# A gated feed-forward and convolution kernel: LoRA products ahead of block 0's transposes, shared statistics, P1 in halves, and other places for the sums

## Chip, cores and metric

The kernel runs on one core of a Trainium2 chip. The metric is the device time of one execution in microseconds (us), the median of several runs. The engines are named as the profile names them: PE is TensorE (PEld its weight loads), DVE VectorE, ACT ScalarE, POOL GpSimd, SP SyncE, whose queue here only issues transfers.

## What is computed

x is 2 x 1024 rows of 512 float32 numbers. Shortened from the reference:

```python
def lora_linear(x, w, a, b):                       # rank 16, SCALING = 2
    return x @ w.T + (x @ a.T) @ b.T * SCALING

xn = layernorm(x)                                  # over the last axis, 512
s = convolve(xn, K) + D * xn                       # K: 512 taps, from 64 complex states
h1, h3 = lora_linear(xn, w1, A1, B1), lora_linear(xn, w3, A3, B3)   # 512 -> 1376
g = silu(h1) * h3
f = lora_linear(g, w2, A2, B2)                     # 1376 -> 512
out = x + s * silu(f)
```

Everything is float32. A product of a 128x128 block by 512 columns is two matmul instructions on PE.

## The kernel before

**Tiles.** The 2048 tokens are four blocks of 512 (TB), each of four tiles of 128. Two blocks form a superblock. The hidden size 1376 is five pairs of chunks (2 x 128, NPAIR) and a last chunk of 96 rows. LoRA is merged into the weights: small products of the rank-16 factors (lora_product, L362) go to a PSUM bank, and merge (L373) adds them to the weight tile on DVE. The factors lie in two halves of the hidden axis, split at 768 (LSPLIT).

**Fast matrix products.** The first layer is done with seven products in place of eight (a Strassen-Winograd form), over two levels for the pairs. A Chain (L719) is seven products P1 to P7 over sums of weights and sums of tokens; the order of the steps is that of the list PLACES (L41): P1, P6, P2, P7, P5, P3, P4. x, w and y are PSUM banks (two of each): P1 starts x, ACT copies x to w, P2 adds to w; P6 and P5 add to x, and ACT takes snapshots (21 and 22) of it; P7 starts y; total(22) adds y to snapshot 22 on DVE; P3 adds to x, P4 to y, and total(21) adds y to snapshot 21. So P4 may not start before total(22) has read y, and y comes free after total(21). Each pair has seven chains (pair_chains, L809; orders, L969), and the last chunk has one for each superblock (last_chain, L793). What a chain delivers is added to other chains' results (plus, L822: DVE for the h1 part, POOL for the h3 part); a Gate (L768) applies silu on ACT and multiplies on POOL, and store_g writes g to DRAM.

**Sums.** Token sums are made on DVE: outer_token_sum (L301, four for each superblock) and inner_token_sum (L317, four names, each for the raw part, raw=True, 1536 elements, and for the sums, 2048 elements). Weight sums: outer_weight_sums (L400) and inner_weight_sum (L409), on DVE; last_sums on POOL.

**Order of the work.** All of the first layer is laid out by hand on a time axis. at(place, what) puts a step into a heap, and after(delay, what) puts one behind the present place; the loop at L1179 takes the steps out in order of place and issues their instructions. One place is about one product of PE. Each engine works its instructions in that order and waits for what an instruction needs. add_chain (L897) puts the seven steps of chain n at 7n + place. SOON (L42) is PLACES with P4 at 11 and not at 13. SP's transfers are issued in the order in which the program has them, at most eight under way at a time.

**The beginning** (L909 to L956 and the first places). SP loads block 0's tiles, block 1, the last chunk's weights, pair 0, blocks 2 and 3, pair 1. ACT's queue issues four LoRA transfers of half 1, loads its function table (warm, L916), then issues those of half 0. PE multiplies the identity by itself (keep_warm, 24 products whose result nobody reads), makes the last chunk's LoRA products, more keep_warm, and transposes block 0 by two tiles. DVE makes the statistics of block 0 (norm_stats, L228), the inverse root (newton_rsqrt, L45: 10 steps, with norm_root's own two 12), then block 1's statistics. normalize (L272) works on ACT (tiles 0 and 2) and POOL (1 and 3). Then come P1 and P2 of the last chain, pair 0's LoRA products between them, block 1's transposes, and the first pair chain. Block 2's statistics are made on DVE at places -6 to -3.6, block 3's on ACT (act_sums, act_squares) with POOL.

**Second layer.** Eight units (unit, L1239) of two token tiles each read g back (load_g, L1078) and multiply with w2 in the same seven-product form; the first two run in turns (run, L1324). Their first product adds chunks of g in order; the last chunks land last. The convolution is multiplied in from unit 4 on.

## Time and profile before

| | us |
|---|---|
| median of three runs | 466.6 (466.06 to 467.17) |
| the profiled execution's own time | 465.92 |
| its span in the trace | 464.1 |
| PE busy | 451.9 |
| DVE busy | 290.3 |
| POOL busy | 194.4 |
| ACT busy | 136.3 |
| first matmul of a chain starts at | 14.26 |
| first matmul of the second layer starts at | 288.52 |

The granted clock of PE is 1.00 in the profile. Durations and places in time come from the one profiled execution, from the start of its span. In a row of the timeline the first number is the start, the second the length of the merged row, then engine, line, operation, what is written and read, and the shape; a bracket gives the engine's idle time before it and what released it. In a row of waits: who waited for whom, us in total, times, the longest. A row of windows has the stretch, its length, then busy time and count for PE, PEld, DVE, ACT and POOL, the granted clock, DMA share and GB/s. A line number can be that of a helper: L709 is every product of a chain.

### The profile page before, as it was taken

What the parts mean: (1) busy time and instruction counts of PE and PEld (TensorE: products, weight loads), DVE (VectorE), ACT (ScalarE), POOL (GpSimd) and SP (SyncE); (2) the same over time, 40 slices, a digit from 0 to 9 for tenths busy, and PEclk for the clock granted to TensorE, in tenths of its full rate; (3) what the DMA queues carried; (4) which work ended last, traced back from release to release, by engine and by line L of the source; (5) the groups of instructions that cost most, each with busy time, mean ns of one, the idle gap of its engine ahead of it and who ended that gap; (6) DMA issues with size and microseconds to landing.
All of it is one profiled execution on the core that took longest, in us unless ns stands there. A gap on an engine that the chain in (4) does not pass through costs nothing.

```text
span 464.1 us, 5003 instructions
## 1 busy us (share of the span) xinstructions
PE 451.9 (97%) x1682; PEld 274.9 (59%) x1682; DVE 290.3 (63%) x494; ACT 136.3 (29%) x281; POOL 194.4 (42%) x156
## 2 busy tenths in 40 slices
PE   8999898989999999999999999999999999999996
PEld 8635333334433443344333344888889898999895
DVE  5898979664776477547745586959786123442222
ACT  2675242433234334432442133111111101111110
POOL 2324262497559555945693359500000112222221
PEclk9999999999999999999999999999999999999999
DMA  8910312015102410241036229296901842422211
GB/s 249 359 43 18 130 57 84 0 54 174 46 23 69 137 45 23 69 151 44 23 98 220 80 83 269 91 333 214 347 1 47 287 139 91 137 90 92 80 57 45
DMA packets 35049, 53.36 MB, mean 115 GB/s; under 512 B 4528, under 2 KB 21168, under 8 KB 34896
## 3 DMA queue, kind: packets, MB, share of 16 engines
q1 hardware_dynamic: 34768, 52.74, 34.6%
q10 hardware_dynamic: 256, 0.31, 0.2%
q8 instruction: 13, 0.21, 0.2%
q14 instruction: 12, 0.10, 0.1%
HBM read 33.64 MB, written 19.40 MB: 114 GB/s over the span
## 4 chain that ended last, share of the span: by engine, by line
PE 83%; DVE 8%; DMA 3%; ACT 2%; POOL 2%; issue 1%; SPq 0%; POOLq 0%
PE x L709 39%; PE y L709 21%; PE w L709 11%; PE aux L881 6%; PE aux L364 2%; PE aux L489 2%; DMA room<-g_dram 2%; DVE s L419 1%; DMA s<-in_x_dram 1%; DVE xt L310 1%; DVE s L733 1%; DVE w L407 1%; DVE t_in L326 1%; POOL s L790 1%; PE w L881 1%
## 5 line engine op out<-in xcount | busy, mean ns | idle before, releaser
L1236 POOL TENSOR_TENSOR o<-o,xin 128x512 f32<-128x512 f32 (+1 forms) x17 | 22.5, 1324 | 140.1 <-DVE o L1235 140.1
L790 POOL TENSOR_TENSOR s<-c,s 128x512 f32<-128x512 f32 (+1 forms) x44 | 59.6, 1356 | 23.2 <-ACT c L782 20.7
L729 ACT COPY s<-x 128x512 f32<-128x512 f32 (+1 forms) x54 | 31.6, 586 | 95.4 <-PE x L709 95.2
L709 PE MATMUL x<-t_in,s 128*128 128x512 f32 (+1 forms) x148 | 56.5, 504 | 0.0
L733 DVE TENSOR_TENSOR s<-s,y 128x512 f32<-128x512 f32 (+1 forms) x54 | 36.5, 681 | 24.1 <-PE y L709 14.4
L823 POOL TENSOR_TENSOR ua_three<-ua_three,s 128x512 f32<-128x512 f32 x20 | 29.8, 1489 | 34.9 <-DVE s L733 34.9
L709 PEld LDWEIGHTS x<-t_in,s 128*128 128x128 f32 x148 | 26.4, 189 | 21.8 <-issue 13.8
L823 POOL TENSOR_TENSOR s<-ua_three,s 128x512 f32<-128x512 f32 x18 | 29.8, 1653 | 21.5 <-DVE s L733 21.5
L709 PE MATMUL y<-t_in,s 128*128 128x256 f32 (+1 forms) x108 | 36.2, 461 | 1.4 <-DVE s L733 1.4
L1257 ACT COPY z<-x 128x256 f32<-128x256 f32 x24 | 8.9, 373 | 83.5 <-PE x L709 83.5
L782 ACT ACTIVATE c<-c 128x512 f32<-128x512 f32 x40 | 25.1, 632 | 12.7 <-DVE c L823 12.7
L709 PEld LDWEIGHTS y<-t_in,s 128*128 128x128 f32 x108 | 20.0, 190 | 13.4 <-issue 8.5
L823 POOL TENSOR_TENSOR s<-u_three,s 128x512 f32<-128x512 f32 x20 | 26.6, 1332 | 0.8
L747 ACT COPY w<-x 128x512 f32<-128x512 f32 (+1 forms) x37 | 21.5, 581 | 8.5 <-PE x L709 8.5
L881 PE MATMUL aux<-conv,xr 128*128 128x128 f32 (+1 forms) x128 | 23.2, 314 | 0.0
L709 PE MATMUL x<-xt,w 128*128 128x512 f32 x40 | 21.0, 607 | 0.7 <-ACT w L747 0.7
L709 PE MATMUL x<-t_in,w 128*128 128x512 f32 x40 | 21.3, 613 | 0.4 <-ACT w L747 0.4
L823 POOL TENSOR_TENSOR u_three<-ua_three,u_three 128x512 f32<-128x512 f32 x10 | 13.3, 1326 | 19.8 <-DVE u_three L733 17.9
L709 PE MATMUL x<-xr,w 128*128 128x512 f32 x40 | 20.8, 615 | 0.6 <-ACT ua_three L729 0.5
L1234 DVE TENSOR_TENSOR aux<-aux,m 128x256 f32<-128x256 f32 x16 | 6.9, 431 | 23.1 <-PE aux L881 23.1
L709 PE MATMUL x<-xr,s 128*128 128x512 f32 x40 | 20.6, 614 | 0.7 <-ACT s L729 0.7
L709 PE MATMUL y<-xt,w 128*128 128x512 f32 x40 | 19.9, 595 | 1.4 <-DVE s L733 1.4
(271 smaller groups left out, 871.5 us busy)
## 6 DMA issues: line engine op xcount, KB each, us to landing
g_dram<-s SPq DMA_DIRECT2D x40, 256.0 KB, 2.1
g<-g_dram SPq DMA_DIRECT2D x10, 512.0 KB, 5.7
xin<-in_x_dram SPq DMA_DIRECT2D x16, 256.0 KB, 2.7
out_dram<-o SPq DMA_DIRECT2D x14, 256.0 KB, 2.0
t_in<-g_dram SPq DMA_DIRECT2D x6, 512.0 KB, 4.2
w<-in_w1T_dram SPq DMA_DIRECT2D x10, 256.0 KB, 3.6
w<-in_w3T_dram SPq DMA_DIRECT2D x10, 256.0 KB, 4.4
s<-in_x_dram SPq DMA_DIRECT2D x8, 256.0 KB, 4.2
```

The source lines that it names most:

```text
L364: nc.tensor.matmul(ps, lhsT=d[:, dc * P : (dc + 1) * P], rhs=h, start=start, stop=True, skip_group_check=True,)
L489: nc.tensor.matmul(ps, lhsT=h, rhs=d, start=True, stop=True)
L709: nc.tensor.matmul(ps, lhsT=lhsT, rhs=rhs, start=first and i == 0, stop=i == len(pairs) - 1, skip_group_check=True,)
L729: nc.scalar.copy(t, self.x)
L733: nc.vector.tensor_tensor(t, t, self.y, add)
L747: nc.scalar.copy(self.w, self.x)
L782: nc.scalar.activation(c, c if src is None else src, AF.Silu)
L790: nc.gpsimd.tensor_tensor(g, act, g, mult)
L823: (nc.vector if o < 20 else nc.gpsimd).tensor_tensor(to, a, b, add)
L881: nc.tensor.matmul(to, lhsT=x_, rhs=by, start=start, stop=True, skip_group_check=True)
L1236: (nc.vector if last else nc.gpsimd).tensor_tensor(o, o, self.xin[h][:, cols], add)
L1257: nc.scalar.copy(t, xb)
```

## The change

- The LoRA factors of half 1 are issued on ACT after the table load, those of half 0 on SP after all other loads. The pairs of the hidden axis are worked in a rotated order (PAIR_AT), and the first two then lie in half 1; w2 is loaded in three pieces in that order (CHUNK_AT).
- keep_warm: 12 products in place of 24 ahead of the LoRA products, 4 later in place of 11. The first LoRA group of pair 0 comes ahead of block 0's transposes, into banks x and w, and its second group between P1 and P2 of the last chain.
- Block 0's tile 1 gets its statistics on ACT and POOL (act_tile); DVE does the others. The inverse root has 8 steps in place of 10. Tile 0 is normalized on DVE.
- The first last chain's P1 is made in two halves of 256 tokens. Token sums of superblocks are made in two halves.
- Block 2's statistics go from places -6 to -3.6 to -1.4 to 1.1; two of block 3's squares to 1.7 and 1.8. P2 of the first pair chain goes from -1.8 to -6.
- In pair 0 the chains 2 to 5 use PLACES in place of SOON. Token sums 1 and 4 of superblock 1, the inner token sums, pair 1's outer weight sums and all inner weight sums 2 and 4 go to later places.
- The gate of the one chain that is held back (early3) and the h3 sum into it go from POOL to DVE.
- At the end of the first layer the P4 of one chain goes from place 13 to 13.5; the first two units of the second layer leave the last chunk of their first product to a second step (wait).

The diff, cut to its core:

```diff
+PAIR_AT = [2 * P * ((c + 3) % NPAIR) for c in range(NPAIR)]
+CHUNK_AT = [PAIR_AT[fc // 2] + fc % 2 * P for fc in range(LAST)] + [LAST * P]
...
-def newton_rsqrt(nc, pool, v, shape):
+def rsqrt(nc, pool, v, shape):
...
-        y.bitcast(I32), v.bitcast(I32), -0.5, float(0x5F3759DF), ALU.mult, ALU.add
+        y.bitcast(I32), v.bitcast(I32), -0.5, float(0x5F1FFFF9), ALU.mult, ALU.add
     )
-    for _ in range(3):
-        nc.vector.tensor_tensor(t, y, y, ALU.mult)
-        nc.vector.scalar_tensor_tensor(t, t, -0.5, v, ALU.mult, ALU.mult)
-        nc.vector.scalar_tensor_tensor(y, t, 1.5, y, ALU.add, ALU.mult)
+    nc.vector.tensor_tensor(t, y, y, ALU.mult)
+    nc.vector.scalar_tensor_tensor(t, t, -c2, v, ALU.mult, ALU.mult)
+    nc.vector.scalar_tensor_tensor(y, t, c2 * 2.38924456, y, ALU.add, ALU.mult)
+    nc.vector.tensor_tensor(t, y, y, ALU.mult)
+    nc.vector.scalar_tensor_tensor(t, t, 1.0 / part**2, v, ALU.mult, ALU.mult)
+    nc.vector.scalar_tensor_tensor(t, t, -10.0 / 3.0, t, ALU.add, ALU.mult)
+    nc.vector.scalar_tensor_tensor(y, t, 5.0, y, ALU.add, ALU.mult)
...
+    def act_tile(b, tt):
+        one = slice(tt, tt + 1)
+        act_sums(b, tt)
+        act_means(b, one)
+        act_squares(b, tt)
+        act_variances(b, one)
...
-                nc.gpsimd.tensor_scalar(t, t, rstd[:, one], shift[:, one], mult, add)
+                engine = nc.vector if tt in on_vector else nc.gpsimd
+                engine.tensor_scalar(t, t, rstd[:, one], shift[:, one], mult, add)
...
-        nc.vector.tensor_tensor(t[name - 1], one, other, add if name == 2 else sub)
+        for k in range(2):
+            to, a, b = (v[:, k] for v in (t[name - 1], one, other))
+            nc.vector.tensor_tensor(to, a, b, add if name == 2 else sub)
...
+            engine = nc.vector if early3 else nc.gpsimd
...
-                        plus(o, held[o], held[o], ua)
+                        nc.vector.tensor_tensor(held[o], held[o], ua, add)
...
-            return Chain(pairs, P, keep, got)
+            return Chain(pairs, P, keep, got, 0.7 if (c, j) == (NPAIR - 1, order[5]) else 0)
...
+    nc.scalar.activation(warm, warm, AF.Silu)
     load_lora(factors, nc.scalar, (1,))
-    nc.scalar.activation(warm, warm, AF.Silu)
-    load_lora(factors, nc.scalar, (0,))
...
     w_pair[1] = load_pair(1)
+    load_lora(factors, nc.sync, (0,))
...
-        keep_warm(ps, 12, True)
+        keep_warm(ps, 6, True)
     ps_last = lora_last()
+    merge_pair(0, w_pair[0], 0, ("x", "w"), (-10.6, -10.5))
     mv = norm_tile(0)
-    norm_stats(0, range(NTT))
+    act_tile(0, 1)
+    norm_stats(0, (0, 2, 3))
     norm_root(mv, 0)
-    normalize(0)
-
-    for i in range(2):
-        keep_warm(primed[1], (5, 2)[i])
-        transpose(0, range(2 * i, 2 * i + 2))
+    mv = norm_tile(1)
+    normalize(0, (2,), (0,))
     keep_warm(primed[1], 4)
-    mv = norm_tile(1)
+    transpose(0, range(NTT))
     norm_stats(1, range(2))
     merge_last(w_last, ps_last, 0)
     norm_stats(1, range(2, NTT))
-    norm_root(mv, 1)
-    merge_last(w_last, ps_last, 1)
...
-        ((1, -11), (2, -8), (7, -2), (6, 1.6), (5, 5.6), (3, 8.6), (4, 11.6)),
+        ((1, -11), (2, -10), (7, -2), (6, 1.6), (5, 5.6), (3, 8.6), (4, 11.6)),
...
-        ((1, -4), (2, -1.8), (7, 3.6), (6, 4.6), (5, 7.6), (3, 10.6), (4, 13.6)),
+        ((1, -8.7), (2, -6), (7, 3.6), (6, 4.6), (5, 7.6), (3, 10.6), (4, 13.6)),
...
-        add_chain(n + 2, pair_chain(0, n), SOON if n < 6 else PLACES)
+        add_chain(n + 2, pair_chain(0, n), PLACES)
...
+            if (c, n) == (NPAIR - 1, 5):
+                places = (*PLACES[:-1], (4, 13.5))
...
-    at(-10, lambda: normalize(1))
-    at(-9.9, lambda: last_sums(w_last, s_last))
-    at(-9, lambda: merge_pair(0, w_pair[0], 0))
-    at(-3.8, lambda: merge_pair(0, w_pair[0], 1))
+    at(-10.9, lambda: norm_root(mv, 1))
+    at(-10.8, lambda: normalize(1))
+    at(-10.7, lambda: merge_last(w_last, ps_last, 1))
+    at(-10.6, lambda: last_sums(w_last, s_last))
+    at(-10.4, lambda: merge_pair(0, w_pair[0], 1, places=(-9.9, -9.8)))
...
-        at(-6 + i, lambda i=i: transpose(1, range(2 * i, 2 * i + 2), "y"))
+        at(-9 + 0.5 * i, lambda i=i: transpose(1, range(2 * i, 2 * i + 2), "y"))
...
-        at(-6 + 0.8 * tt, lambda tt=tt: norm_stats(2, (tt,)))
+        at((-1.4, 0.2, 1, 1.1)[tt], lambda tt=tt: norm_stats(2, (tt,)))
...
-        at(-0.3 + 0.1 * tt, lambda tt=tt: act_squares(3, tt))
+        at((-0.3, -0.2, 1.7, 1.8)[tt], lambda tt=tt: act_squares(3, tt))
...
-    for name, when in ((3, 15.7), (2, 15.9), (1, 17.3), (4, 18.4)):
+    for name, when in ((3, 15.7), (2, 15.9), (1, 21.2), (4, 21.4)):
...
-        (3, True, 20.3),
-        (3, False, 21.5),
-        (2, True, 23.4),
-        (2, False, 25.4),
-        (1, True, 35.6),
-        (1, False, 38.2),
-        (4, True, 40.6),
-        (4, False, 43),
+        (3, True, 21.6),
+        (3, False, 22.8),
+        (2, True, 24.2),
+        (2, False, 27),
+        (1, True, 37),
+        (1, False, 40.3),
+        (4, True, 47.3),
+        (4, False, 51.3),
...
-                    14.5 + 0.2 * n if c == 0 else t1 + 8.5 + 1.5 * n,
+                    (44.3, 45.1, 52.4, 53.2)[n] if c == 0 else t1 + 8.5 + 1.5 * n,
...
-                (2, ready(5) + 1),
-                (4, max(ready(3), ready(5) + 2)),
+                (2, ready(5) + 4),
+                (4, max(ready(3), ready(5) + 8)),
...
-        mul(xb, a11, b11, True)
+        if wait:
+            pairs = [t[:, c, cut] for t in a11 for c in range(t.shape[1])]
+            pairs = list(zip(pairs, b11))
+            product(xb, pairs[:-1], True)
+            yield
+            product(xb, pairs[-1:], False)
+        else:
+            mul(xb, a11, b11, True)
...
-    run([unit(0, read), unit(1, read)], [*t[:2], *s1, *s4_, *t[2:], *more], 4, 4)
+    run([unit(u, read, wait=True) for u in range(2)], [*t[:2], *s1, *s4_, *t[2:], *more], 4, 5)
```

More of the change, by code (lines that the diff above doesn't have):

```diff
@@ L42 @@
 SOON = ((1, 0), (6, 3), (2, 4), (7, 5), (5, 6), (3, 9), (4, 11))
-def newton_rsqrt(nc, pool, v, shape):
+def rsqrt(nc, pool, v, shape):
     y = pool.tile(shape, F32, tag="rs_y", name="rs_y")
     t = pool.tile(shape, F32, tag="rs_t", name="rs_t")
+    part = 3.0 / 8.0
+    c2 = part * 0.703952253
     nc.vector.tensor_scalar(
-        y.bitcast(I32), v.bitcast(I32), -0.5, float(0x5F3759DF), ALU.mult, ALU.add
+        y.bitcast(I32), v.bitcast(I32), -0.5, float(0x5F1FFFF9), ALU.mult, ALU.add
     )
-    for _ in range(3):
-        nc.vector.tensor_tensor(t, y, y, ALU.mult)
-        nc.vector.scalar_tensor_tensor(t, t, -0.5, v, ALU.mult, ALU.mult)
-        nc.vector.scalar_tensor_tensor(y, t, 1.5, y, ALU.add, ALU.mult)
+    nc.vector.tensor_tensor(t, y, y, ALU.mult)
[5 more added lines that the diff above has]
+    nc.vector.scalar_tensor_tensor(y, t, 5.0, y, ALU.add, ALU.mult)
     return y
@@ L210, in load_x @@
     def load_x(b):
-        room = (None, None, t_in[4], t_in[6])[b]
-        tiles = []
-        for tt in range(NTT):
-            t = value() if room is None else room[:, tt, :]
-            nc.sync.dma_start(out=t, in_=x[bass.ds(b * TB + tt * P, P), :])
-            tiles.append(t)
+        room, tiles = (None, None, t_in[4], t_in[6])[b], []
+        n = 1 if room is None else 2
+        for tt in range(0, NTT, n):
+            to = value().unsqueeze(1) if room is None else room[:, tt : tt + n, :]
+            rows = x[bass.ds(b * TB + tt * P, n * P), :]
+            nc.sync.dma_start(out=to, in_=rows.rearrange("(k p) d -> p k d", p=P))
+            tiles += [to[:, k, :] for k in range(n)]
         return tiles
@@ L235, in act_sums @@
     def act_sums(b, tt):
-        if tt == 0:
+        if b not in sums_of_x:
             sums_of_x[b] = small.tile([P, 3, NTT], F32, tag="act_sums", name="act_sums")
@@ L240, in act_sums, with act_means @@
         )
-    def act_means(b):
-        sums = sums_of_x[b]
-        nc.gpsimd.tensor_scalar(sums[:, 1, :], sums[:, 0, :], -1.0 / DIM, None, mult)
-        nc.gpsimd.tensor_scalar(norms[b][:, :, 0], sums[:, 0, :], 1.0 / DIM, None, mult)
+    def act_means(b, tiles=slice(0, NTT)):
+        s, neg, _ = (sums_of_x[b][:, i, tiles] for i in range(3))
+        nc.gpsimd.tensor_scalar(neg, s, -1.0 / DIM, None, mult)
+        nc.gpsimd.tensor_scalar(norms[b][:, tiles, 0], s, 1.0 / DIM, None, mult)
     def act_squares(b, tt):
@@ L255, in act_squares, with act_variances @@
         )
-    def act_variances(b):
+    def act_variances(b, tiles=slice(0, NTT)):
         nc.gpsimd.tensor_scalar(
-            norms[b][:, :, 1], sums_of_x[b][:, 2, :], 1.0 / DIM, None, mult
+            norms[b][:, tiles, 1], sums_of_x[b][:, 2, tiles], 1.0 / DIM, None, mult
         )
+    def act_tile(b, tt):
[4 more added lines that the diff above has]
+        act_variances(b, one)
     def norm_root(mv, *blocks):
@@ L265, in norm_root @@
         nc.vector.tensor_scalar(veps, mv[:, :, 1], EPS, None, add)
-        rstd = newton_rsqrt(nc, small, veps, [P, n])
+        rstd = rsqrt(nc, small, veps, [P, n])
         shift = small.tile([P, n], F32, tag="shift", name="shift")
@@ L270, in norm_root, with normalize @@
             norms[b] = [t[:, n * NTT : (n + 1) * NTT] for t in (rstd, shift)]
-    def normalize(b, on_act=(0, 2)):
+    def normalize(b, on_act=(0, 2), on_vector=()):
         rstd, shift = norms[b]
@@ L381, in load_pair @@
                 slot = (1, 2, 0, 3)[2 * v + half]
-                rows = src[half * HALF : (half + 1) * HALF, 2 * c * P : 2 * (c + 1) * P]
+                rows = src[half * HALF : (half + 1) * HALF, PAIR_AT[c] : PAIR_AT[c] + 2 * P]
                 nc.sync.dma_start(
@@ L387, in load_pair, with merge_pair @@
         return w
-    def merge_pair(c, w, half, tag="aux"):
-        ps = [bank(tag), bank(tag)]
+    def merge_pair(c, w, half, tags=("aux", "aux"), places=None):
+        ps = [bank(tag) for tag in tags]
         for k in range(2):
@@ L394, in merge_pair @@
                 n = slice(k * 2 * P, (k + 1) * 2 * P)
-                lora_product(ps[v][:, n], v, 2 * half + k, 2 * c * P, 2 * P, k == 0)
+                lora_product(ps[v][:, n], v, 2 * half + k, PAIR_AT[c], 2 * P, k == 0)
         for v in range(2):
             to = w[:, (1, 2, 0, 3)[2 * v + half]].rearrange("p k m h -> p (k m h)")
-            after(1.6 + v, lambda to=to, v=v: merge(to, ps[v]))
+            when = places[v] if places else now[0] + 1.6 + v
+            at(when, lambda to=to, v=v: merge(to, ps[v]))
     def outer_weight_sums(w, names):
@@ L470, in load_w2 @@
         w2["b"] = const.tile([P, 3, DIM], F32, tag="w2b", name="w2_b")
-        nc.sync.dma_start(
-            out=w2["a"], in_=w2T[: 8 * P, :].rearrange("(c p) d -> p c d", p=P)
-        )
-        nc.sync.dma_start(
-            out=w2["b"][:, :2], in_=w2T[8 * P : LAST * P, :].rearrange("(c p) d -> p c d", p=P)
-        )
+        for c in range(0, LAST, 4):
+            to = w2["a"][:, c : c + 4] if c < 8 else w2["b"][:, :2]
+            n = to.shape[1] * P
+            rows = w2T[CHUNK_AT[c] : CHUNK_AT[c] + n, :]
+            nc.sync.dma_start(out=to, in_=rows.rearrange("(c p) d -> p c d", p=P))
         nc.sync.dma_start(out=w2["b"][:LASTR, 2], in_=w2T[LAST * P :, :])
@@ L487, in merge_down @@
             ps = aux()[:rows, :]
-            d, h = lora_factors(0, 1, fc * P, rows)
+            d, h = lora_factors(0, 1, CHUNK_AT[fc], rows)
             nc.tensor.matmul(ps, lhsT=h, rhs=d, start=True, stop=True)
@@ L704, in s4_matrix, with product, __init__ @@
         yield
-    def product(ps, pairs, first):
-        for i, (lhsT, rhs) in enumerate(pairs):
-            nc.tensor.matmul(
-                ps,
-                lhsT=lhsT,
-                rhs=rhs,
-                start=first and i == 0,
-                stop=i == len(pairs) - 1,
-                skip_group_check=True,
-            )
+    def product(ps, pairs, first, parts=1):
+        n = ps.shape[1] // parts
+        for part in range(parts):
+            cols = slice(part * n, (part + 1) * n)
+            for i, (lhsT, rhs) in enumerate(pairs):
+                nc.tensor.matmul(
+                    ps[:, cols],
+                    lhsT=lhsT,
+                    rhs=rhs if parts == 1 else rhs[:, cols],
+                    start=first and i == 0 and part == 0,
+                    stop=i == len(pairs) - 1,
+                    skip_group_check=True,
+                )
     class Chain:
-        def __init__(self, pairs, rows, keep, got, late=0):
+        def __init__(self, pairs, rows, keep, got, late=0, parts=1):
             self.pairs, self.rows, self.keep, self.got = pairs, rows, keep, got
-            self.late = late
+            self.late, self.parts = late, parts
         def snapshot(self, o):
@@ L743, in step @@
             to = self.w if i == 2 else self.y if i in (7, 4) else self.x
-            product(to, self.pairs(i), i in (1, 7))
+            product(to, self.pairs(i), i in (1, 7), self.parts if i == 1 else 1)
             if i == 1:
@@ L768, in s4_gated_ffn, with __init__ @@
     class Gate:
-        def __init__(self, rows, chunk, sb):
-            self.rows, self.chunk, self.sb, self.c = rows, chunk, sb, {}
+        def __init__(self, rows, chunk, sb, engine=nc.gpsimd):
+            self.rows, self.chunk, self.sb, self.c, self.engine = rows, chunk, sb, {}, engine
         def put(self, o, c, src=None):
@@ L789, in pair_up @@
                     g, act = self.c.pop(three), self.c.pop(one)
-                    nc.gpsimd.tensor_tensor(g, act, g, mult)
+                    self.engine.tensor_tensor(g, act, g, mult)
                     store_g(g, self.rows, self.chunk, self.sb, low)
@@ L805, in got @@
                 gate.put(o, c)
-        return Chain(pairs, LASTR, lambda o: value(), got, 1)
+        return Chain(pairs, LASTR, lambda o: value(), got, 1, 2 if sb == 0 else 1)
     def pair_chains(c, w, s, order):
@@ L825, in chain @@
         def chain(j):
+            early3 = j == 3 and order.index(3) < order.index(5)
+            engine = nc.vector if early3 else nc.gpsimd
             gate = (
-                Gate(P, 2 * c + (j in (5, 4)), int(j in (5, 3))) if j in (2, 5, 3, 4) else None
+                Gate(P, 2 * c + (j in (5, 4)), int(j in (5, 3)), engine)
+                if j in (2, 5, 3, 4)
+                else None
             )
-            early3 = j == 3 and order.index(3) < order.index(5)
             if early3:
@@ L991, in s4_gated_ffn @@
             hurry = (c, n) in ((NPAIR - 2, 6), (NPAIR - 1, 4))
-            add_chain(2 + 7 * c + n, pair_chain(c, n), SOON if hurry else PLACES)
-    at(-10, lambda: normalize(1))
-    at(-9.9, lambda: last_sums(w_last, s_last))
-    at(-9, lambda: merge_pair(0, w_pair[0], 0))
-    at(-3.8, lambda: merge_pair(0, w_pair[0], 1))
+            places = SOON if hurry else PLACES
+            if (c, n) == (NPAIR - 1, 5):
+                places = (*PLACES[:-1], (4, 13.5))
+            add_chain(2 + 7 * c + n, pair_chain(c, n), places)
+    at(-10.9, lambda: norm_root(mv, 1))
[3 more added lines that the diff above has]
+    at(-10.4, lambda: merge_pair(0, w_pair[0], 1, places=(-9.9, -9.8)))
     for i in range(2):
-        at(-6 + i, lambda i=i: transpose(1, range(2 * i, 2 * i + 2), "y"))
+        at(-9 + 0.5 * i, lambda i=i: transpose(1, range(2 * i, 2 * i + 2), "y"))
     for n, name in enumerate((3, 2, 1)):
@@ L1004, in s4_gated_ffn @@
     for tt in range(NTT):
-        at(-6 + 0.8 * tt, lambda tt=tt: norm_stats(2, (tt,)))
+        at((-1.4, 0.2, 1, 1.1)[tt], lambda tt=tt: norm_stats(2, (tt,)))
         at(-1.4 + 0.1 * tt, lambda tt=tt: act_sums(3, tt))
-        at(-0.3 + 0.1 * tt, lambda tt=tt: act_squares(3, tt))
+        at((-0.3, -0.2, 1.7, 1.8)[tt], lambda tt=tt: act_squares(3, tt))
     at(-0.9, lambda: act_means(3))
-    at(0.2, lambda: act_variances(3))
+    at(1.9, lambda: act_variances(3))
     at(6.9, lambda: norm_root(mv_late, 2, 3))
@@ L1015, in s4_gated_ffn @@
         at(place, lambda b=b, i=i: transpose(2 + b, range(2 * i, 2 * i + 2)))
-    for name, when in ((3, 15.7), (2, 15.9), (1, 17.3), (4, 18.4)):
+    for name, when in ((3, 15.7), (2, 15.9), (1, 21.2), (4, 21.4)):
         at(when, lambda name=name: outer_token_sum(1, name))
-    at(19.4, spill)
+    at(22.5, spill)
     for name, when in ((1, 12.7), (2, 13.4), (4, 14), (3, 33.3)):
@@ L1237, in result, with unit @@
             nc.sync.dma_start(out=out[self.rows[h], cols], in_=o)
-    def unit(u, read, held=None):
+    def unit(u, read, held=None, wait=False):
         a11, a12, a22, s1, s2, s3, s4_, gl = read
```

## Prediction

> **What bounds the kernel now.** I read the page's busy times first, then the chain that ended last, TensorE's waits, and the timeline around the longest of them.

> ```profile
> PE 451.9 (97%) x1682; PEld 274.9 (59%) x1682; DVE 290.3 (63%) x494; ACT 136.3 (29%) x281; POOL 194.4 (42%) x156
> ```

> TensorE (PE) sets the time. In a run without waits, 512-column matmuls start 0.43 us apart, so one product of 128x128 by 512 (two matmuls) takes 0.86, a product of the last chain (two row blocks) 1.72. Only the beginning, waits, and work that can be left out can be won. The chain in order of time shows the beginning:

> ```profile
> 2.10 4.69 DMA s<-in_x_dram
> ...
> 6.81 0.70 DVE stats L231
> ...
> 9.93 0.17 DVE shift L268
> 10.12 0.82 ACT s L277
> ...
> 12.53 1.00 PE aux L288 x8
> 13.53 0.89 PE w L927 x8
> 14.42 1.74 PE x L709 x4
> ```

> The fourth tile of block 0 lands at 6.78, VectorE's (DVE) statistics and root end at 10.1, and the first chain product starts at 14.3. PE's waits:

> ```profile
> PE y L709 <- DVE s L733: 2.7, 2, 1.4
> PE w L927 <- POOL ident masks.py:199: 1.4, 1, 1.4
> PE x L709 <- ACT s L729: 1.3, 2, 0.7
> PE x L709 <- ACT w L747: 1.1, 2, 0.7
> PE x L709 <- ACT ua_three L729: 0.5, 1, 0.5
> PE x L709 <- DMA room<-g_dram: 0.4, 1, 0.4
> ```

> Between starts of matmuls (start to start, less 0.43 or 0.21) these cost a little more: 0.80 at 29.2, 1.52 at 52.5, 1.54 at 76.7, 0.57 at 89.7, 2.10 together at 96.4 to 104.4, 0.84 at 285.4, 0.58 at 290.0: 7.95 in all. From 108 to 280 there is none of note. The timeline shows what the longest are:

> ```profile
> 50.93 1.22 DVE L310 TENSOR_TENSOR xt<-xr,xt 128x1024 f32<-128x1024 f32 x1
> ...
> 52.07 1.75 DVE L322 TENSOR_TENSOR t_in<-xr 128x1536 f32<-128x1536 f32 x1
> ...
> 53.74 0.68 DVE L733 TENSOR_TENSOR s<-s,y 128x512 f32<-128x512 f32 x1
> 54.47 1.13 PE L709 MATMUL y<-xt,w 128*128 128x512 f32 x2 [1.36 <-DVE s L733]
> ```

> P4 adds into bank y, which total(22) must have read first; that addition stood in DVE's queue behind token sums. By stage:

> ```profile
> 52.00:81.30 29.30, 26.57 (x61) 10.28 (x60) 26.13 (x22) 8.51 (x15) 13.89 (x8) 1.00 0.17 56
> ```

> DVE (third) is busy 26.1 of 29.3 us: a second bound.

> **The beginning.** The four LoRA transfers on ScalarE's (ACT) queue go behind the table load (1.28) and the other four behind all loads. Block 0's tiles land at 3.66 to 6.78 now; later tiles, with less between them, 0.75 apart (7.46, 8.21). So the fourth lands between 3.66+3x0.75=5.9 and 6.8: I take 6.1. ACT's tile, from its rows for block 3 (0.64+0.20 sums, 0.23 POOL, 0.71+0.19 squares, 0.25 POOL), takes 2.1 from 4.4 on and is done at 6.5; DVE's last tile ends at 6.1+0.95=7.05. The root has 10 steps of 0.197 instead of 12: it ends at 9.1, not 10.1. DVE normalizes tile 0: no row of that form; TENSOR_SCALAR 128x512 on DVE (L533) took 0.48, between 0.3 and 0.8; I take 0.45. ACT copies (0.57) and two aux banks then pace the transposes: the fourth tile's end at 11.9. P1 in halves needs tiles 0 and 1 alone for its first half (tiles 2 and 3 are copied during it), and merge_last(0), on DVE at 9.55+2x0.81+0.46=11.6. So P1 starts at 11.9, not 14.3; 4 more matmuls of half the width cost no columns. Eight LoRA matmuls (1.1) now run near 8, in idle time. P2 ends at 16.3, not 19.1.

> Block 1: DVE needs 4x0.81 for statistics, 0.46, 1.97 for the root: 15.2, not 16.1. Normalizing, transposes and eight copies (0.27 apart, as now) end at 20.1, not 22.2. Token sum 3 in halves lets P7 start 0.7 later: 20.85 instead of 23.60, with a pair product (0.86) more behind it: 3.6 ahead. Here something else is late. Block 2's statistics stood in DVE's wait for this block; now they stand behind it: from 20.1, eight half sums x0.61, four statistics x0.81, four weight sums x0.66, root 2.0, two merges x0.61 make 14.0: 34.1. The second LoRA group of pair 1 needs the aux banks that those merges free; PE would be there at 32.4 and leaves it at 34.9, now 37.2. **2.3 is won** (3.4 if DVE keeps up; 1.5 if the tile lands at 6.8).

> [...] Against the halves: [...] The row: 1.22 against 0.68 long, but back to back they start 1.14 and 0.61 apart, so 0.08 more. For the four sums here that is [...]0.3 by the row; I use the row. Against halving the warm-up: [...] The trace's warm-up has 14 matmuls in 3.0 us, then 15 and 16 in each 1.5. After the change 24 of them end near 5.6 and the LoRA factors land near 7: 1.4 idle, [...]so I count 0[...]. No row shows such a gap.

> **Block 2/3 and pair 0.** The 52.5 wait: total(22) now stands ahead of token sums 1 and 4: **-1.5**. Next late: the P4 of the last chain on the second half. Its total follows, from 44.75 on: four token sums 4.9, inner sums 3 and 2 1.7+2.2+1.7+2.2, and four additions 2.6: 60.1 (61.2 if one sum takes 2.82, as L324 did beside GpSimd), PE there at 59.9: **+0.8**. The 76.7 wait: both parts of inner sum 4 (1.74+2.28) stood ahead of a total; now the total is ahead of both and done at 73.9, PE at 75.4: **-1.5**. Pair 1's four weight sums (2.7) leave the crowd before 47 for 75 to 84. P4 two places later closes y for 1.7 longer; P7 of the chain after next still comes five products later, 4.3 against 0.9 needed.

> At 90 to 104: POOL is busy 12.6 of 12.8 us; the held sums and gates of chain 3 move to DVE: four of 1.27 to 2.0 off POOL, four of 0.68 onto DVE. Inner weight sums 2 and 4 go 3 and 6 places later, past the totals they delayed (98.0 and 100.6). The first wait (copy to w behind two Silus, 0.57) stays, and with DVE fuller I add **0.5** (0 to 0.9); of the other 2.1 I take **-1.3** (0 to 2.1).

> At 285: one product (0.86) now stands between P5 and P3, the wait was 0.84. At 290: the other unit's first products (8x0.21=1.7) stand before the last chunk, the wait was 0.58, moved up by the 0.84. **-1.3** (0.7 to 1.4).

> At nothing: LoRA's half 0 on SP's queue (four issues ahead of the first spill; first read past 100 us, since the rotated order begins in half 1), w2 in three loads (the one load of 2 MB lands at 249.97 and keeps DVE 0.95, PE nothing; its halves land no later), x by two tiles (same bytes). Without that cover each costs a landing, 2 to 4 us. The 0.8 at 29.2, a snapshot behind four squares on ACT, is within the 2.3: two squares now stand behind it.

> Sum: -2.3-1.5+0.8-1.5+0.5-1.3-1.3 = **-6.6**. The profiled execution took 465.92 (span 464.1 and 1.8 around it), so 459.3; the median of the runs is 0.7 above it: **460.0**.

> **Rivals.** *All waits go* (DVE keeps up everywhere): -2.3-3.06-2.67-1.42=-9.45: 457.1. For it: DVE has 35% free from 107 to 280. *The clock falls*: 462.5. *DVE stays the bound*: what leaves 52 to 104 comes back at other products, only the beginning and the end are won: 463.0. For it: 26.1 of 29.3. *Slower*: sums placed later run beside GpSimd's additions of 79 on. L324's 2.82 for a 128x1536 sum whose like took 1.75 is a factor of 1.6. On the eight inner sums (18 us of rows with L328's) and the weight sums (2.7) that is up to 12 more; past 2 of slack PE waits for all of it: 470.0. It decides from 9.5 of stretch on (2 of slack, 6.6 won, 0.9 to be seen). Against it: only two of eight sums were stretched. That the change doesn't do what it says is excluded: the built order has each move.

> **Numbers.** Forecast 55%, 458 to 462.3. All waits go 20%, clock 10%, DVE bound 8%, no change 3%, slower 4%. A measurement of this kernel tells 0.2% (0.9 us) from nothing. Faster 93%, same 3%, slower 4%. The range goes from the low end of the bounds (-10.5, the beginning at 3.4) to their high end (-2.9): 456.0 to 463.8.

> **What would show it.** P1 near 11.9 (wrong above 13); PE at the end of pair 1's second LoRA group near 35; no wait of PE for DVE s of 1.4; a new wait before the last chain's P4 below 1.3; the copy to w behind Silu stays; no PE wait on room<-g_dram. Matmuls 0.2 apart beyond 6 us would be the clock. If DVE is busy over 95% of the stretch 45 to 80 and PE waits on it as before, the bound was DVE.

## The result and the profile after

| | before | after |
|---|---|---|
| median of 4 runs | 466.33 us (465.71 to 467.17) | 474.19 us (469.89 to 475.0) |
| profiled execution, span | 465.92, 464.1 | 475.0, 473.2 |
| first chain product (P1) | 14.26 | 18.40 |

The changed kernel is slower: ratio 1.0146, 95% interval 1.0111 to 1.018. Executions of one kernel here differ more than before the change, as their mean TensorE clock differs (0.981 in the profiled run, 0.993 in that of 469.89): a profile shows one course, the median decides.

The page of the changed kernel, its busy times and the clock that was granted in each fortieth of the span:

```profile
PE 455.6 (96%) x1648; PEld 277.1 (59%) x1648; DVE 293.4 (62%) x499; ACT 137.3 (29%) x284; POOL 192.2 (41%) x155
...
PEclk8798999989999999999999999999999999999999
```

PE has fewer matmuls (1648 against 1682) and is busy for longer: some ran slowly. The clock is below full in slices 1, 2, 4 and 9 (11.8 us each). The chain of waits at the start, in order of time (start, duration):

```profile
1.16 3.59 DMA s<-in_x_dram
4.75 0.02 issue
4.77 4.50 DMA lo_h<-in_b3T_dram
9.27 0.04 issue
9.31 1.80 PE y L386 x13
...
13.09 2.00 PE w L957 x8
15.09 3.51 PE aux L308 x16
18.61 1.80 PE x L735 x8
```

A LoRA transfer, not block 0, now leads. It is issued at 4.77, which was 2.10 before: the four LoRA transfers are now issued behind the table load in the program, so that in the built order the last of them takes the completion counter of block 0's second tile and waits for that tile, which lands at 4.75. The LoRA transfer itself lands at 9.27 instead of 6.67. (There are eight such counters in the traces of both kernels, and the transfers of SP and of ACT take them in turn: the eight under way at a time are shared by both queues, and a transfer of one can wait for one of the other. In the kernel before, one of SP's loads of x waited 1.0 for a LoRA transfer of ACT.) Then eight warm-up matmuls (L957) take 2.00, sixteen transposes (L308) 3.51. In the chain of before, at full clock, eight warm-up matmuls took 0.89 and eight transposes 1.00. The stages of the changed kernel (window, length, busy time and count for PE, PEld, DVE, ACT and POOL, then PEclk, DMA share and GB/s):

```profile
6.00:8.00 2.00, 0.40 (x3) 0.24 (x2) 1.78 (x6) 0.81 (x2) 0.57 (x3) 1.00 1.07 386
8.00:10.00 2.00, 0.69 (x6) 0.69 (x8) 1.69 (x10) 0.28 (x1) 0.21 (x1) 0.59 1.12 268
10.00:18.00 8.00, 8.00 (x43) 6.80 (x42) 7.11 (x23) 1.93 (x4) 3.55 (x5) 0.50 1.08 363
...
42.00:46.00 4.00, 3.64 (x5) 1.42 (x6) 3.62 (x5) 0.89 (x2) 1.45 (x2) 0.57 0.00 0
...
97.00:101.00 4.00, 3.79 (x5) 1.70 (x6) 1.93 (x5) 0.74 (x2) 3.17 (x3) 0.57 0.00 0
```

PEclk is the third number from the right. Three stretches of half clock stand out: 8.4 to 18.6, 42.5 to 45.9 and 97.1 to 100.5. PE's waits of the changed kernel (total, times, longest):

```profile
PE x L735 <- ACT w L773: 3.5, 2, 2.1
PE y L735 <- DVE s L759: 3.0, 2, 1.9
PE y L386 <- DMA lo_h<-in_b3T_dram: 2.9, 1, 2.9
...
PE y L735 <- DVE xt L332: 0.8, 1, 0.8
PE y L735 <- DVE w L431: 0.8, 1, 0.8
PE aux L386 <- DVE w L396: 0.6, 1, 0.6
```

The waits at 52.5, 76.7, 285 and 290 are gone. New ones, start to start as in the prediction: 3.10 at 6.1, 0.98 at 26.3, 0.92 at 30.7, 0.81 and 0.56 at 39 to 42, 1.22 at 68.9 (the last chain's P4), 2.24 at 94.5, 1.60 at 104.6, 2.11 at 108.9. At the same product the changed kernel is late by 4.1 at P1, 5.2 behind pair 1's second LoRA group, 6.9 after the half clock to 46, about 4.9 behind the place of the old 76.7 wait, 9.7 from 112 to 280, and 9.1 at the end.

### The profile page after: what moved, and what is told of

It is laid out like the page before. It is cut to its first block, busy times and chain, and to the rows that moved or that the text cites. A ratio compares the mean times of both kernels' runs of the same rounds, so it can differ in the third digit from the quotient of the medians.

```text
span 473.2 us, 4956 instructions
## 1 busy us (share of the span) xinstructions
PE 455.6 (96%) x1648; PEld 277.1 (59%) x1648; DVE 293.4 (62%) x499; ACT 137.3 (29%) x284; POOL 192.2 (41%) x155
## 4 chain that ended last, share of the span: by engine, by line
PE 82%; DVE 10%; issue 3%; DMA 2%; ACT 2%; POOL 1%; SPq 0%; DVEq 0%; POOLq 0%; ACTq 0%
PE x L735 38%; PE y L735 20%; PE w L735 10%; PE aux L911 6%; DVE xt L332 2%; PE aux L512 2%; PE aux L386 2%; PE aux L308 1%; DVE w L431 1%; DVE s L759 1%; DMA lo_h<-in_b3T_dram 1%; DVE t_in L346 1%; DVE t_in L344 1%; DMA s<-in_x_dram 1%; PE w L911 1%
## 5 line engine op out<-in xcount | busy, mean ns | idle before, releaser
L816 POOL TENSOR_TENSOR s<-c,s 128x512 f32<-128x512 f32 (+1 forms) x42 | 57.5, 1372 | 28.2 <-ACT c L808 25.9
L755 ACT COPY s<-x 128x512 f32<-128x512 f32 (+1 forms) x54 | 31.6, 584 | 94.7 <-PE x L735 94.5
L849 POOL TENSOR_TENSOR ua_three<-ua_three,s 128x512 f32<-128x512 f32 x20 | 27.0, 1348 | 36.0 <-DVE s L759 36.0
L735 PEld LDWEIGHTS x<-t_in,s 128*128 128x128 f32 x148 | 26.4, 190 | 21.8 <-issue 13.8
L849 POOL TENSOR_TENSOR s<-ua_three,s 128x512 f32<-128x512 f32 x18 | 28.3, 1571 | 22.4 <-DVE s L759 22.4
L849 POOL TENSOR_TENSOR s<-u_three,s 128x512 f32<-128x512 f32 x20 | 30.2, 1511 | 0.8
L735 PEld LDWEIGHTS y<-t_in,s 128*128 128x128 f32 x108 | 20.0, 190 | 11.7 <-issue 8.7
L735 PE MATMUL x<-t_in,w 128*128 128x512 f32 x40 | 22.2, 638 | 2.1 <-ACT w L773 2.1
L849 POOL TENSOR_TENSOR u_three<-ua_three,u_three 128x512 f32<-128x512 f32 x10 | 15.6, 1558 | 20.9 <-DVE u_three L759 20.9
L735 PE MATMUL x<-xt,s 128*128 128x512 f32 x40 | 20.8, 603 | 0.0
```

Source lines behind the costliest of these rows:

```text
L735: nc.tensor.matmul(ps[:, cols], lhsT=lhsT, rhs=rhs if parts == 1 else rhs[:, cols], start=first and i == 0 and part == 0, stop=i == len(pa ...
L755: nc.scalar.copy(t, self.x)
L816: self.engine.tensor_tensor(g, act, g, mult)
L849: (nc.vector if o < 20 else nc.gpsimd).tensor_tensor(to, a, b, add)
```

## The experiments

Theories. **Clock**: the late transfer and the halved warm-up drop the clock, and the rest follows. **VectorE is the bound** (rival): the places moved make DVE late between 22 and 111, and the start alone matters little. A third came up on the way: the held sums and gates of chain 3, moved from POOL to DVE, block DVE's queue.

| run | built from | median us | ratio to before, 95% | P1 at |
|---|---|---|---|---|
| e1_warm24 | after | 470.48 | 1.0053 to 1.0101 | 14.99 |
| e2_lane | after | 468.61 | 1.0006 to 1.0054 | 13.85 |
| e3_before_halfwarm | before | 468.21 | 1.0014 to 1.0038 | 15.85 |
| e4_warm24_lane | after | 469.87 | 1.0047 to 1.0081 | 13.83 |
| e5_gates_pool | e4 | 466.54 | 0.9984 to 1.0006 | 14.97 |
| e6_sum4_back | e4 | 467.95 | 1.0021 to 1.0052 | 14.17 |
| e7_before_tail | before | 465.17 | 0.9949 to 0.9985 | 14.91 |
| e8_start_alone | e4 | 470.11 | 1.0040 to 1.0085 | 14.30 |
| e9_both_back | e4 | 464.48 | 0.9934 to 0.9964 | 14.30 |
| e10_no_keep_warm | e9 | 465.07 | 0.9940 to 0.9976 | 13.91 |
| e11_before_totals | e7 | 464.89 | 0.9940 to 0.9975 | 14.90 |
| e12_filler | e5 | 467.71 | 0.9992 to 1.0030 | 14.84 |
| e13_filler_37 | e10 | 464.03 | 0.9914 to 0.9953 | 12.98 |
| e14_before_moves | e11 | 463.56 | 0.9908 to 0.9956 | 14.41 |
| e15_low_rows | before | 467.69 | 1.0000 to 1.0044 | 15.91 |

The kernel before, run beside them, had medians of 466.53 to 466.93. P1 is from the profiled run. With the full warm-up it moves by up to 1.1 with the moment at which the warm-up comes to full clock (in the profile of the kernel before its matmuls start 0.21 apart up to 4.6, and 0.11 from there on): in e4 that is at 4.9, the LoRA products start at 8.61 and P1 follows 5.2 later; in e5 it is at 7.3 and 9.74, and P1 again follows 5.2 later.

**The start.** e1 puts the warm-up back:

```diff
-        keep_warm(ps, 6, True)
+        keep_warm(ps, 12, True)
```

> The changed kernel with the warm-up put back to two times twelve (48 matmuls instead of 24); the late fourth LoRA transfer stays. Clock theory: the warm-up ends near 8.6 and PE waits only 0.7 us for the transfer that lands at 9.3, the clock stays full, P1 starts at about 13 instead of 18.4; 474.2 less 5.2 for the start (the offset at the end of pair 1's second LoRA group) is 469, and 466 if the half clock at 42 to 46 and 97 to 101 goes as well. Rival, VectorE is the bound: the start is won but given back as waits on VectorE between 40 and 111, and the time stays above 472.

e2 puts the LoRA transfers ahead of the table load again:

```diff
+    load_lora(factors, nc.scalar, (1,))
     nc.scalar.activation(warm, warm, AF.Silu)
-    load_lora(factors, nc.scalar, (1,))
```

> The changed kernel with the four LoRA transfers issued ahead of the table load, as before the change; the halved warm-up stays. In the built order the fourth then no longer waits for block 1's first tile. Clock theory: it lands near 6.5, PE waits 0.6 us instead of 2.9, the clock stays full, P1 starts near 12.3, and the time is 465 to 468. Rival, VectorE is the bound: above 471. A third case, that the halved warm-up alone drops the clock: P1 after 15.

(The tile waited for is block 0's second, not block 1's first, as that text has it.) e3 is the kernel before with `keep_warm(ps, 6, True)` in place of 12.

> The kernel before with only the warm-up halved; there all LoRA factors land by 6.7. Clock theory: PE waits 0.7 us from 6.0 on, the clock stays full, and since the transposes wait for block 0 anyway, P1 stays at 14.3 and the time at 466.3, within 0.5. If the number of warm-up matmuls itself decides the clock: half speed behind it, P1 near 17, and 468 to 470.

e4 has both edits of e1 and e2.

> The changed kernel with both put back: the full warm-up and the LoRA transfers ahead of the table load. Clock theory: no wait of PE for the factors; LoRA products from 8.6 on, P1 near 12.6, within 0.5 us of the run with the earlier transfers alone, 465 to 468. Rival, VectorE is the bound: above 471, with waits on VectorE for y and of PE for the copy to w between 90 and 111 as in the changed kernel.

Each edit of the start brings P1 from 18.4 to 14 or 15, and 3.7 to 5.6 us of the median. So the start costs some 4.3 (474.19 to 469.87 with both), as the clock theory has it. How much of it is the transfer and how much the warm-up is not told: e2 alone has a lower median than both edits together, but its twelve times fall into two groups, 467.0 to 467.5 and 469.7 to 470.9. The times lie between the two theories, and e4, whose clock is full from 5 to 100, is still 3.1 above before: the clock at the start is not all.

e2 has what the forecast assumed, factors that land early and a halved warm-up; its LoRA products start at 6.79, without a wait. Its clock falls all the same, at 10.4:

```profile
8.00:10.00 2.00, 1.98 (x17) 1.40 (x14) 1.69 (x10) 0.27 (x1) 0.20 (x1) 1.00 1.17 318
10.00:12.00 2.00, 1.67 (x8) 1.54 (x8) 1.93 (x6) 1.09 (x2) 1.59 (x2) 0.60 1.10 329
12.00:14.00 2.00, 2.00 (x11) 1.76 (x10) 1.90 (x6) 1.21 (x3) 0.00 (x0) 0.55 1.10 368
```

My expectation for e2, that the clock stays full, failed with it. e3 failed as well: PE waited 2.34 at 8.6 for block 0, half clock followed from 11.7 to 15.2, P1 came 1.6 late and the median 1.4 above its before. So the second half of the warm-up does not fill time alone: with it the granted clock was 1.00 while block 0 was awaited (before), without it 0.50 from 11.7 on (e3).

**What is left in e4.** DVE in e4's timeline, with the idle time ahead of an instruction and its releaser in brackets:

```profile
91.21 0.68 DVE L759 TENSOR_TENSOR s<-s,y 128x512 f32<-128x512 f32 x1
93.95 0.69 DVE L894 TENSOR_TENSOR s<-s,ua_three 128x512 f32<-128x512 f32 x1 [2.07 <-POOL ua_three L849]
94.56 0.68 DVE L849 TENSOR_TENSOR ua_one<-ua_one,x 128x512 f32<-128x512 f32 x1
95.16 0.68 DVE L849 TENSOR_TENSOR c<-u_one,x 128x512 f32<-128x512 f32 x1
...
97.14 1.38 DVE L816 TENSOR_TENSOR s<-c,s 128x512 f32<-128x512 f32 x1 [0.70 <-ACT c L808]
...
102.09 0.69 DVE L894 TENSOR_TENSOR s<-s,ua_three 128x512 f32<-128x512 f32 x1 [1.37 <-POOL ua_three L849]
102.81 1.64 DVE L816 TENSOR_TENSOR s<-c,s 128x512 f32<-128x512 f32 x1
```

DVE stands still for 2.07, 0.70 and 1.37, for POOL and ACT: the held sum (L894) needs ua_three, which POOL still adds, and the gate (L816) needs ACT's Silu. Behind them stand the adders ua_one and c, behind c the next Silu, and behind that on ACT the copy to w for which PE waits 1.56 at 98.8. e5 takes both operations back to POOL:

```diff
-            engine = nc.vector if early3 else nc.gpsimd
+            engine = nc.gpsimd
...
-                        nc.vector.tensor_tensor(held[o], held[o], ua, add)
+                        plus(o, held[o], held[o], ua)
```

> The changed kernel with full warm-up and early LoRA transfers, and chain 3's held sums and gates back on GpSimd. In the run with those two starts VectorE waited 2.07 us at 91.9 and 1.37 at 100.7 for GpSimd's ua_three, because the held sum stood in its queue, and PE lost 0.61+0.78+1.73 between 94.8 and 100.3 and another 2.1 at half clock after it. Theory (the moved sums block VectorE's queue): these go, at most 1.5 as before the change is left, and the median falls by 3 to 4, from 469.9 to near 466.3; the wait of 2.24 at 88 stays, since its adders stand ahead of them. Rival (GpSimd then is late, as it was busy 12.6 of 12.8 us there before): the same loss turns up as PE waiting on work behind GpSimd, and the time stays within 1 of 469.9.

466.54: 3.3 less, as expected. The adders now follow total without a wait, in e5's timeline:

```profile
92.32 0.67 DVE L759 TENSOR_TENSOR s<-s,y 128x512 f32<-128x512 f32 x1
92.91 0.67 DVE L849 TENSOR_TENSOR ua_one<-ua_one,x 128x512 f32<-128x512 f32 x1
93.51 0.67 DVE L849 TENSOR_TENSOR c<-u_one,x 128x512 f32<-128x512 f32 x1
```

Of the waits of 0.61, 0.78 and 1.73 one of 1.19 is left. The wait of 2.24 stays. It is for the copy to w, which on ACT stands behind two Silus that need c; ahead of c, DVE's queue in e4 holds inner sum 4 and an outer weight sum (L431):

```profile
82.63 2.97 DVE L348 TENSOR_TENSOR t_in<-xt,t_in 128x2048 f32<-128x2048 f32 x1
85.53 0.68 DVE L849 TENSOR_TENSOR u_one<-ua_one,x 128x512 f32<-128x512 f32 x1
86.13 1.76 DVE L431 TENSOR_TENSOR w<-w 128x512 f32<-128x512 f32 x2
87.81 0.67 DVE L849 TENSOR_TENSOR ua_one<-ua_one,w 128x512 f32<-128x512 f32 x1
88.41 0.68 DVE L849 TENSOR_TENSOR c<-u_one,w 128x512 f32<-128x512 f32 x1
```

e6 moves inner sum 4 and pair 1's outer weight sums back:

```diff
-        (4, True, 47.3),
-        (4, False, 51.3),
+        (4, True, 40.6),
+        (4, False, 43),
...
-                    (44.3, 45.1, 52.4, 53.2)[n] if c == 0 else t1 + 8.5 + 1.5 * n,
+                    14.5 + 0.2 * n if c == 0 else t1 + 8.5 + 1.5 * n,
```

> The changed kernel with full warm-up and early LoRA transfers, and inner token sum 4 and pair 1's four outer weight sums back at their places of before. Theory (the wait of 2.24 at 88 is these sums, moved from where they were): it goes, a wait of 1.5 comes back near 75, and some of the 0.8 to 1.0 waits before 40 grow; net within 1 of 469.9. Rival (the new places are a gain): the old waits come back and the one at 88 stays, 471.5 to 473.

467.95, 1.9 less: the 2.24 falls to 0.57 as before the change, 1.26 comes back at 79, the new wait at 63 grows from 1.23 to 1.48, and nothing grew before 40. e9 has the edits of e5 and e6 together.

> The changed kernel with full warm-up and early LoRA transfers, and both later parts undone: chain 3's held sums and gates on GpSimd, inner sum 4 and pair 1's outer weight sums at their old places. If the two losses are separate they add: 469.9 less 3.3 less 1.9 is 464.6. If they are one loss (the same products late), 466 to 466.5.

464.48: the two losses add.

**Gains taken alone.** e7 is the kernel before with the end of the change (its last lines in the diff, the place 13.5 and the 0.7 later totals).

> The kernel before with the change's end alone (the last chunk of P1 in a step of its own, s4's stores at 5, and P4 of the last pair's chain 5 at 13.5 with its totals 0.7 later). The forecast has it at -1.3 (0.7 to 1.4): both waits at 285 and 290 gone, 465.5 against 466.8. Rival: the waits move to the next product, within 0.3 of before.

-1.4, both waits gone. e8 is e4 with all places behind the beginning, P4 of pair 0, the gates and the end put back as before.

> The changed kernel's beginning alone, with full warm-up and early LoRA transfers: all places of token and weight sums behind it, P4 of pair 0's chains, chain 3's gates and the end are as before. P1 near 13.8. If the start is worth what the forecast gave it once the clock holds: 2.3 less, 464.5. If VectorE sets the end of pair 1's second LoRA group anyway (37.34 in the run with the same start against 37.28 before): 466.8, within 0.7, with waits of PE on VectorE's sums at 22 to 37.

470.11 (four runs), 3.6 above before: worse than both expectations. PE waits 0.98, 0.92, 0.79 and 0.56 at 22 to 38 as in e4, 2.15 at 53.5 (1.52 before), and in this profile half clock follows at 57 to 60 and, with no wait ahead, at 262 to 265. e10 is e9 without the line `keep_warm(primed[1], 4)`.

> The run before it with the four warm-up matmuls between the LoRA products and block 0's transposes left out, so that the transposes and P1 come up to 0.9 earlier. If VectorE sets the beginning (block 1's statistics, root and sums), PE waits 0.9 longer for the sums near 23 and the time is within 0.4 of the run before it. If PE does, 0.9 less.

P1 comes 2.27 behind the end of its LoRA group, 3.20 in e9: 0.93 won. PE's waits on DVE didn't grow (0.98, 0.92, 0.80, 0.56), so DVE does not set the beginning by its load: each of these waits is a return path (PE's transpose or product, ACT's copy, DVE's sum, PE again) that moves with PE. (They are the same in e5, with P1 at 14.97; and in e4 DVE itself stands still for 2.93 up to 22.2, for ACT's last copy of block 1.) The lowest run is 0.9 below e9's (462.64 against 463.57), but half clock at 37.8 to 41.2 takes 1.7 of the profiled run (0.39 ahead of e9 at 37.8, 1.27 behind it at 41.3), and the median is 0.6 above. e11 puts the middle on e7:

```diff
-        add_chain(n + 2, pair_chain(0, n), SOON if n < 6 else PLACES)
+        add_chain(n + 2, pair_chain(0, n), PLACES)
...
-    for name, when in ((3, 15.7), (2, 15.9), (1, 17.3), (4, 18.4)):
+    for name, when in ((3, 15.7), (2, 15.9), (1, 21.2), (4, 21.4)):
```

and the spill, inner sums 3, 2 and 1 at the change's places.

> The kernel before with the change's end and the middle's moves alone: P4 of pair 0's chains two places later, outer token sums 1 and 4 and the inner sums 1 to 3 later, inner sum 4, all weight sums and the gates as before. The forecast has -1.5 for the wait at 52.5 and +0.8 for the next one: 465.2 less 0.7, 464.5. If VectorE is the bound there, the wait of 1.5 moves to the last chain's P4 in full (1.48 in the run with sum 4 put back): 465.2 within 0.3.

464.89, not told apart from e7; in the profile 1.52 at 52.5 became 1.43 at 62.7, the 1.53 at 77 became 1.26, and the 0.87 at 97 grew to 1.22. e14 adds the change's later inner weight sums 2 and 4 to it:

```diff
-                (2, ready(5) + 1),
-                (4, max(ready(3), ready(5) + 2)),
+                (2, ready(5) + 4),
+                (4, max(ready(3), ready(5) + 8)),
```

> The kernel before with the change's end and the middle's moves, and with inner weight sums 2 and 4 at the change's places as well; beginning, inner sum 4, outer weight sums and gates as before. In that run without them PE lost 0.66 at 103.5 (before: the same 0.66), which the runs with the new places don't show: 464.9 less 0.7, 464.2. If VectorE only shifts the wait: 464.9.

463.56, the 0.66 at 103.5 gone. It has the lowest median, 0.9932 (0.9908 to 0.9956) of before, though this interval overlaps those of e7, e9 and e11: beginning, gates, inner sum 4 and outer weight sums of before, with the end, P4's places, token sums and inner weight sums of the change.

**The clock.** e12 fills e5's wait at 89.8:

```diff
+    at(58.5, lambda: keep_warm(bank("aux"), 8, True))
```

> The changed kernel with full warm-up, early LoRA transfers and chain 3's gates on GpSimd, and eight identity matmuls (1.7 us) into a free bank placed ahead of the product that waits 2.07 us at 89.8; nothing else of it changes. If that wait is what drops the clock (512-column matmuls 0.85 apart from 93.3 to 95.8, 1.26 lost), it stays full and the time falls by 1.2, to 465.3. If the wait doesn't set the clock, the time stays at 466.5 or above.

The clock held: 512-column matmuls stay 0.43 apart there, and the wait falls to 0.45, so the product at 93.71 is 1.26 ahead of e5, and the next one 1.80. But the next copy to w is as late as ever: that wait grows from 1.19 to 2.88, and from there the products are where they were (115.38 against 115.49). The median is 467.71, above e5's, with intervals that overlap. What the filler won was given back within 10 us. e13 puts `at(8.85, lambda: keep_warm(bank("w"), 3, True))` into e10; its filler is written to a bank of the ring of w in which a sum is open, which changes part of that sum, so e13 speaks for the time alone.

> The run without the four warm-up matmuls (465.07 median, 462.64 lowest), with three identity matmuls of 128 rows (0.65 us) placed ahead of pair 1's second LoRA group, where PE waits 0.64 for VectorE. If the clock fell at 38.8 because the 3.3 us before it held waits of 1.0 and 1.7 of 16-row products, it falls less often: no half clock at 38 to 41, median near 463.5, lowest as before. If the filler is too small or the cause another: 465.

464.03, and no half clock at 38 to 41 in its profile. The intervals overlap e10's, so this is in favour and not proof. e15 keeps every matmul of before and changes the rows of half the warm-up:

```diff
-    for ps in primed:
-        keep_warm(ps, 12, True)
+    for ps, rows in zip(primed, (P, R)):
+        keep_warm(ps, 12, True, rows)
```

with `ident[:rows, :]` for both operands.

> The kernel before with the second twelve of the 24 warm-up calls on 16 rows of the identity instead of 128 (warm-up values are not used); same number of matmuls, same columns, no wait more. If 16-row matmuls count as little work for the clock: half clock from about 8.5 to 12 on the LoRA products and the transposes behind them, P1 1 to 2 us later, 467.5 to 468.5. If only being busy counts: P1 and time as before, 466.5 within 0.4.

The stages of e15 (columns as above):

```profile
6.00:8.00 2.00, 2.00 (x18) 1.88 (x17) 1.83 (x5) 0.00 (x0) 0.00 (x0) 1.00 1.04 369
8.00:10.00 2.00, 2.00 (x29) 2.00 (x27) 1.65 (x11) 0.00 (x0) 0.00 (x0) 0.87 1.09 249
10.00:12.00 2.00, 2.00 (x12) 1.83 (x11) 1.90 (x7) 1.52 (x2) 1.52 (x2) 0.50 1.23 260
12.00:14.00 2.00, 2.00 (x16) 2.00 (x15) 1.93 (x5) 0.67 (x2) 0.00 (x0) 0.77 1.09 308
```

and the same of the kernel before:

```profile
8.00:10.00 2.00, 2.00 (x25) 1.78 (x25) 1.65 (x11) 0.00 (x0) 0.00 (x0) 1.00 1.07 280
10.00:12.00 2.00, 1.92 (x18) 1.73 (x17) 1.93 (x6) 1.84 (x3) 1.52 (x2) 1.00 1.23 237
```

PE is busy 2.00 of 2.00 in each stage of e15, and the clock falls to 0.50; P1 moves from 14.26 to 15.91 (0.35 of it is there already when the LoRA products start, 8.82 against 8.47, since the warm-up came to full speed later: 11 matmuls from 4 to 6 us, 17 in before). So in e15 the matmuls of 16 rows did not keep the clock, though PE was busy with them.

```profile
34.36:37.78 3.42, 0.68 (x2) 0.00 (x0) 1.00 0.00 0
37.78:41.19 3.41, 3.38 (x4) 1.35 (x5) 0.50 0.00 0
```

In e9 they are spread over two steps, and the clock stays full:

```profile
33.23:36.64 3.41, 2.21 (x6) 0.55 (x4) 1.00 0.00 0
36.64:40.05 3.41, 1.85 (x5) 0.81 (x6) 1.00 0.00 0
```

An estimate from the starts of the matmuls in all 17 profiles, with 0.43 for 512 columns and up to 455 us: of 16 steps at full clock with at most 1.05 us of 128-row matmuls, 15 were followed by half clock (the other is in e1, at 259.5); of 13 with 1.08 to 1.31, five were, and these five held no 16-row matmuls, the eight others 1.3 to 1.7 us of them; of more than 2000 above 1.31, none was. In the changed kernel the three steps ahead of half clock held 0.84, 0.49 and 1.17 us of 128-row matmuls, the last without 16-row matmuls; one with 1.24, and 1.6 of 16-row matmuls, at 261.0, stayed full.

## Why the prediction was wrong, by its steps

460.0 was forecast, 474.19 measured. The terms that failed are the zero for the clock at the start, the -2.3 to be won there, the +0.5 for the copy to w, and the -1.3 for 90 to 104.

- **LoRA factors near 7, "1.4 idle", counted as 0 for the clock.** Failed. The 0 was my estimate: no row showed such a gap. The fourth factor landed at 9.27, since a wait for another transfer came with the new order, which the built order shows beside the DMA and I did not price. PE was idle 2.91, the clock fell at 8.4 and came back at 18.6. The late factor is not all of it: in e2, where nothing was late, the clock fell at 10.4. I counted idle time alone, and the LoRA products, of 16 rows, as work like any other. My rival for the clock, 462.5, put it at 2.5; the start cost some 4.3 in the medians.
- **P1 at 11.9.** Failed even with the clock mended: 13.83 in e4, and 12.98 at best (e13). Root 10.18 instead of 9.1 in e4 (the fourth tile landed at 6.87, not 6.1), and I let ACT's copies pace the transposes, where PE had the 24 LoRA matmuls to 10.6, eight warm-up matmuls to 11.5 and sixteen transposes to 13.8 in its own queue. But e4 has 24 matmuls of warm-up more than the change. In e2, which has not, PE waits from 9.98 to 10.33 for tile 0 (root at 9.7), and its transposes take 3.52 at half clock where e4's take 2.27: with full clock P1 would have come near 12.6 (an estimate). "In idle time" was true of none of the eight LoRA matmuls in e4; in e2 it was, since PE waited for tile 0 behind them.
- **-2.3 at the end of pair 1's second LoRA group.** There e4 is 0.5 late at the product behind it (37.73 against 37.21). Between 22 and 38 return-path waits take 3.26, against 1.27 in before (0.47 at 20.3, 0.80 at 29.2); that is more than P1 (0.43 ahead in e4) and the LoRA products moved out of this stretch (1.06) had won. Block 1's sums could start at 22.2, not at 20.1, and DVE, on which I had this step end, was waiting for them. The halves themselves cost what the row said: they start 0.60 to 0.61 apart.
- **-1.5 at 52.5, +0.8 behind it.** Mechanism right: no wait there, 1.22 at the last chain's P4, under the 1.3 that I gave as its limit; the 0.8 was 0.4 too small.
- **-1.5 at 76.7.** Right: gone in the changed kernel, back as 1.26 in e6. But the sums that left it now stand in DVE's queue at 77 to 88, which is the next step:
- **+0.5 for the copy behind two Silus.** Mis-sized: 2.24 instead of 0.57, so +1.7. Inner sum 4 took 2.98 in the changed kernel (2.97 in e4), while POOL worked on an addition of 3.32, and not 2.28. e6 undoes this for 1.9 in the median.
- **-1.3 for the others at 90 to 104.** This step failed most: I counted the moved sums and gates as 4x0.68 of DVE's time and not as waits. They cost the wait for POOL and for ACT, and all that is queued behind: e5, 3.3 in the median. The other half of the step, the later inner weight sums, held: the 0.66 at 103.5 is gone in e14. (POOL's 12.6 of 12.8 us are of the stretch from 94.2 to 107; from 81.3 to 94.2 it was busy 6.8 of 12.9.)
- **-1.3 at the end.** Right: e7, -1.4.
- **Rivals.** "The clock falls" and "DVE stays the bound" were both at work, and I let neither of them end above the time of before. "Slower" had another mechanism: no stretch of 12 us was seen, DVE's busy time grew from 290.3 to 293.4 in all.

The sum by medians: 474.19, less 4.3 for the start, 3.3 for the gates, 2.1 for sum 4 and the weight sums, is 464.5 (e9); before plus the end and the better places is 463.6 (e14). These two differ by the changed beginning (mended, with its loads and order of pairs) alone: it is worth nothing that these runs show. In the two profiles e9 is 0.1 ahead at P2 of the last chain and 0.8 behind from pair 1's second LoRA group on. Half clock also comes between 257 and 265 in six of the profiles (e7, e8, e9, e10, e13, e14), though PE had no wait there. In e9 the two stages are

```profile
255.00:258.00 3.00, 3.00 (x10) 0.88 (x6) 2.02 (x4) 0.86 (x2) 2.92 (x3) 1.00 0.00 0
258.00:262.00 4.00, 4.00 (x7) 1.16 (x8) 1.85 (x3) 0.00 (x0) 0.45 (x1) 0.57 0.20 66
```

with eight 16-row matmuls (L512) between 254.6 and 258.3. In these six the step ahead held 0.86 to 1.05 us of 128-row matmuls, in the other eleven the poorest step of this stretch 1.15 or more, but for e1: where the raster happens to lie against the 16-row matmuls would then decide. With e15 this makes them the likely cause, but they weren't removed in a run of their own.

## What to carry to other kernels

An operation moved to a less busy engine brings its waits along: list what it needs and who produces that, and what stands behind it in the new queue, before counting its duration. When DMA issues are reordered, read in the built order what each now waits for. A wait on PE costs a second time if half clock follows it (1.7 behind the wait of 2.07 in e5), and covering it wins nothing while the next operand stays late (e12). To judge whether the clock will hold, count the matmuls of many rows, and not the idle time alone (e15: PE busy 2.00 of 2.00, granted clock 0.50).
